# Attention of a pre-norm layer on one core: blocks of 16 queries with 51 keys in place of blocks of 32 with 68, one unit of work per sequence and group

## The chip, the core and the metric

One core of a Trainium2 chip. Its engines are TensorE (PE; the loading of its weights is shown apart as PEld), VectorE (DVE), ScalarE (ACT) and GpSimd (POOL); SyncE (SP) issues all DMAs. Each engine works through its own instructions in order. The metric is the device time of one execution in microseconds. The median of three runs is given, and apart from them one profiled execution, from which all durations come.

## What is computed

A layer for 16 sequences of 256 tokens with 256 channels. Attention has 16 heads of 128 in 4 groups; a group has four query heads and one key and value head. A query sees the 32 newest keys up to itself and the first four of its sequence.

```python
mask = (k <= q) & ((k < 4) | (k >= q - 31))
def attn(x):                                  # x normalised
    q, k, v = x @ wq.T, x @ wk.T, x @ wv.T    # 16, 4 and 4 heads of 128
    scores = einsum('bhtd,bhsd->bhts', q, repeat(k, 4)) / sqrt(128)
    p = exp(where(mask, scores, min) - row_max) * mask
    return einsum('bhts,bhsd->bhtd', p / sum(p), repeat(v, 4)) @ wo.T
x = x + attn(layernorm(x))
x = x + ffn(layernorm(x))     # rows and weights rounded to 8-bit steps, y = x_q @ w_q.T, scaled, + bias
```

All inputs and the output are float32. The four weight matrices of the attention arrive transposed.

## The kernel before

**Units and blocks.** The work of the attention runs in units (n, g, t): sequence, group, and half of the sequence (128 queries). There are 128 of them. A unit has four blocks of 32 queries; a block's four heads give 128 rows of scores. Each block sees 68 keys: the 32 of the block before, its own 32 and the first four. `kt` holds these 68 columns for each block (`keys_to`, L437, four copies on ScalarE), `vw` the matching rows of the values, spread over 96 partitions by DMAs from DRAM (`values_to`, L455).

**What a unit does.** `scores_and_turned` (L561) multiplies queries by keys: one product of 128x128 weights (`qt`) and 68 columns for each block, into `pss`. `mm` (L87) issues every product as two with 64 columns of weights each. VectorE adds the mask (L584) and takes the negative maximum (L586). ScalarE makes four exponentials, 128x68 each (L611), which also give the row sums. VectorE divides (L618, L619, L630) and transposes in 32x32 blocks (L595) into `z`. `z` goes to DRAM (`zd`, L597) and comes back rearranged as `ad` (L601), with keys on 96 partitions. `times_values` (L632) multiplies it by `vw` into `po`, and ScalarE copies `po` to `oT` (L648). The first three units and the last three are turned by TensorE (`ptd`, L578) instead of by way of DRAM.

**Products saved.** Queries, keys, values and the output projection are computed with seven block products in place of eight. GpSimd forms sums of the operands (`left_sums`, `right_sums`, L265 to L275), TensorE multiplies (`products`, L279), and `combine` (L304 to L320) adds the results: on VectorE for queries (`qt`) and the output (`pc`), on GpSimd for keys and values, whose banks ScalarE copies out first (`both_banks`, L333). For queries ScalarE copies one product first (`p_q`, L331). Sequence 0 uses plain products, and so does the output of sequence 15.

**PSUM.** `ps_m` has two banks, which `po`, keys and values and small things share; queries have two (`q0`, `q1`), `py` two, `pss` and `ptd` one each.

**Order.** The loop at L961 goes through the units and writes down each engine's order by hand (`in_written_order`, L21): scores of unit i; products of the output for earlier units; exponentials of i; `po` of the unit whose weights were sent two units ago (`lag`, L854); one of keys or values for the next sequence; division of i; the next queries. Other steps are hung on slots of the loop through `at` (L861): the statistics and transposition of the next sequence (`turned_by_blocks`, L395: four DMAs out, L404, and four back, L413), the FFN of finished sequences (`ffn_steps`, L708), the loads. `hT` (L759) is the FFN's transposed input, copied by ScalarE when its four DMAs `hb` have landed. Before the loop stand the loads (L103 to L115), nine warming products, the first norm, the masks on GpSimd (`mask_steps`), and the first keys, queries and values. After the last unit `last_steps` (L785) does the FFN for the two halves of sequence 15; the first half's steps are placed among the last unit's.

Of the kernel before, what the change touches and what calls it, by code (L numbers as in the profile page):

```python
# [34 lines left out]
def kernel(  # L35
# [25 lines left out]
    QB = 32  # L61
    NBLK = P // QB
    SB = T // QB
    NK = SINK + 2 * QB

    NCH = 3
    NKP = NCH * QB
    assert WIN == QB and HG * QB == P  # L70
# [3 lines left out]
    xp = ctx.enter_context(tc.tile_pool(name="xp", bufs=6))  # L74
# [10 lines left out]
    CT = P // 2  # L85

    def mm(to, left, right, start, stop):  # L87

        for c in range(0, P, CT):
            pe.matmul(to[c : c + CT], left[:, c : c + CT], right, start=start, stop=stop)  # L90

# [14 lines left out]
    wv_sb = const.tile([P, NC, G * D], FP, name="wv_sb")  # L106
    sp.dma_start(wv_sb, wvT.rearrange("(c p) n -> p c n", p=P))
# [4 lines left out]
    for g in range(G):  # L112
        sl = slice(g * HG * D, (g + 1) * HG * D)
        sp.dma_start(wq_sb[:, :, sl], wqT_v[:, :, sl])
    load_x(1)  # L115
# [4 lines left out]
    def other_loads():  # L120

        woT_v = woT.rearrange("(h p) n -> p h n", p=P)
        for g in range(G):
            sp.dma_start(wo_sb[:, g * HG : (g + 1) * HG, :], woT_v[:, g * HG : (g + 1) * HG, :])
        sp.dma_start(wf_sb, wf.rearrange("(c p) d -> p c d", p=P))
        sp.dma_start(bias_bc, bias.partition_broadcast(P))
# [9 lines left out]

    masks = const.tile([P, NT, NBLK, NK], FP, name="masks")
# [4 lines left out]
    floor = const.tile([P, NBLK], FP, name="floor")  # L144
# [4 lines left out]
    def keep(ap, base, cm, step):  # L149

        pool.affine_select(
            out=ap, in_=ap, compare_op=ALU.is_ge, fill=NEG, base=base,
            pattern=[[step, ap.shape[1]]], channel_multiplier=cm,
        )


    scores = [const.tile([P, NBLK, NKP], FP, name=f"scores_{j}") for j in range(2)]
    for j in range(2):
        pool.memset(scores[j], 0.0)

    def mask_steps():


        def build(b):
            pool.memset(masks[:, 0, b, :], 0.0)
            if b < 2:
                pool.memset(masks[:, 0, b, 2 * QB :], NEG)
            if b == 0:
                pool.memset(masks[:, 0, b, 0:QB], NEG)
            for h in range(HG):  # L170
                m = masks[h * QB : (h + 1) * QB, 0, b, 0 : 2 * QB]
                keep(m, QB, 1, -1)
                if b == 1:
                    keep(m[:, SINK:], SINK - 1, -1, 1)
                elif b == 2:
                    keep(m, -1, -1, 1)

        def others():
            like = masks[:, 0, 2:3, :]
            pool.tensor_copy(masks[:, 0, 3:, :], like)  # L180
            pool.tensor_copy(masks[:, 1], like.to_broadcast([P, NBLK, NK]))
            pool.tensor_copy(ident16, ident)
            pool.memset(ones, 1.0)

        return [lambda b=b: build(b) for b in (2, 0, 1)] + [others]
# [22 lines left out]
    def ffn_weight_steps():  # L208
# [23 lines left out]
        def turn():  # L232
            for c in range(NC):
                pt = ps_m.tile([P, NC, P], BF, tag="m", name=f"wt_{c}")
                for o in range(NC):
                    pe.transpose(pt[:, o, :], wq16[:, o, c * P : (c + 1) * P], ident16)
                act.copy(wqfT[:, c, :], pt.rearrange("p o n -> p (o n)"))

        def spread_scales():
            pw = ps_m.tile([P, DM], FP, tag="m", name="pw")  # L240
# [12 lines left out]
    def y_banks(name):  # L253
        return [ps_y.tile([P, NBLK, P], FP, tag=f"y{k}", name=f"{name}_{k}") for k in range(2)]

    def region(p, i):
        return p[REGION[i][0]][:, REGION[i][1]]

    def fast_queries(n, h=0):
        return n > 0 and (n, h) != (B - 1, H - 2)  # L260

    def fast_output(n):
        return 0 < n < B - 1
# [24 lines left out]

    SMALL_FIRST = (4, 5, 3, 1, 2, 6, 7)
    turn_of = [0]

    def q_bank(other, name):
        return ps_q.tile([P, NBLK, P], FP, tag=f"q{turn_of[0] ^ other}", name=name)

    def banks_of_chunk(name):
        p = [ps_m.tile([P, NBLK, P], FP, tag="m", name=f"{name}_0"), q_bank(0, f"{name}_1")]  # L300
        turn_of[0] ^= 1
        return p
# [19 lines left out]
    class Products:  # L322
# [10 lines left out]
        def both_banks(self):  # L333

            copies = [p2.tile([P, 4 - j, P], FP, tag=f"b{j}", name=f"b{j}_{self.tag}") for j in range(2)]
            for k in (1, 0):
# [11 lines left out]

    keys_late = {}
# [19 lines left out]
    def norm_steps(n):  # L369
        def stats():  # L370
            mvs[n] = statistics(xts[n], range(NT), f"a{n}")

        def norm(t):
            if t == 0:
                xns[n] = p1.tile([P, NT, DM], FP, tag="xn", name=f"xn_{n}")
            standardise(xns[n], xts[n], mvs[n], [t])

        return [stats, lambda: norm(0), lambda: norm(1)]
# [7 lines left out]
    def turned(n):  # L386
        xnT[n] = p2.tile([P, NC, T], FP, tag="xnT", name=f"xnT_{n}")
        pt = ps_m.tile([P, NC, T], FP, tag="m", name=f"xt_{n}")
# [5 lines left out]

    def turned_by_blocks(src, pool_of, tag):  # L395


        z = p1.tile([P, NQ, NT * NC, QB], FP, tag="zx", name=f"z_{tag}")
        dve.transpose(z, src.rearrange("p t (c q i) -> p q (t c) i", c=NC, q=NQ))
        zd = dram.tile([P, NQ, NT * NC, QB], FP, tag="zx", name=f"zd_{tag}")  # L400

        def out():
            for a in range(NQ):
                sp.dma_start(  # L404
                    zd[:, a].rearrange("(q j) k i -> j q (k i)", q=NQ),
                    z[a * QB : (a + 1) * QB].rearrange("j q k i -> j q (k i)"),
# [12 lines left out]

    NQ = P // QB  # L420
# [16 lines left out]
    def keys_to(n, g, kb):  # L437

        k = p2.tile([P, 2, SB, NK], FP, tag="kt", name=f"kt_{n}_{g}")
        for e in range(2):  # L440
            kt[n, g + e] = k[:, e]
        act.copy(k[:, :, :, QB : 2 * QB], kb)
        act.copy(k[:, :, 1:, 0:QB], kb[:, :, 0 : SB - 1, :])
        act.copy(k[:, :, 0, 0:QB], kb[:, :, 0, :])
        act.copy(k[:, :, :, 2 * QB :], kb[:, :, 0, 0:SINK].unsqueeze(2).to_broadcast([P, 2, SB, SINK]))

    vws = [const.tile([NKP, SB, 2 * D], FP, name=f"vw_{j}") for j in range(2)]  # L450

    def values_buffer(n, pair):
        vw[n, pair] = vws[pair]

    def values_to(n, pair, v, tiles=range(NT)):  # L455


        w, fresh = vw[n, pair], n == 0
        b0, b1 = tiles[0] * NBLK, (tiles[-1] + 1) * NBLK
        sp.dma_start(w[1:NKP:NCH, b0:b1], v[b0:b1].rearrange("b k d -> k b d"))  # L460
        c1 = min(b1 + 1, SB)
        sp.dma_start(w[0:NKP:NCH, b0 + 1 : c1], v[b0 : c1 - 1].rearrange("b k d -> k b d"))
        if b0 == 0:
            rows = QB if fresh else SINK
            sp.dma_start(w[2 : NCH * (rows - 1) + 3 : NCH], v[0, 0:rows].unsqueeze(1).to_broadcast([rows, SB, 2 * D]))
            if fresh:
                sp.dma_start(w[0:NKP:NCH, 0], v[0])

    def plain_keys(n, g):
        pk = ps_m.tile([P, 2, T], FP, tag="m", name=f"pk_{n}_{g}")  # L470
        for e in range(2):
            for c in range(NC):
                mm(
                    pk[:, e, :], wk_sb[:, c, (g + e) * D : (g + e + 1) * D], xnT[n][:, c, :],
                    start=(c == 0), stop=(c == NC - 1),
                )
        return lambda: keys_to(n, g, pk.rearrange("p e (k i) -> p e k i", i=QB))

    def plain_values(n, t):
        pv = ps_m.tile([P, G * D], FP, tag="m", name=f"pv_{n}_{t}")  # L480
        for c in range(NC):
            mm(
                pv, xnT[n][:, c, t * P : (t + 1) * P], wv_sb[:, c, :],
                start=(c == 0), stop=(c == NC - 1),
            )

        def rest():
            v = p2.tile([P, 3, 2, D], FP, tag="vt", name=f"vt_{n}_{t}")
            act.copy(v[:, 0:2].rearrange("p j e d -> p (j e d)"), pv)
            if t == 0:  # L490
                plain_v.append(dram.tile([T, 2, 2 * D], FP, tag="vp", name=f"vp_{n}"))
                for pair in range(2):
                    values_buffer(n, pair)
            vd = plain_v[0]
            sp.dma_start(vd[t * P : (t + 1) * P].rearrange("p j d -> p (j d)"), v[:, 0:2].rearrange("p j e d -> p (j e d)"))
            for pair in range(2):
                values_to(n, pair, vd[:, pair].rearrange("(b k) d -> b k d", k=QB), [t])
# [4 lines left out]

    def keys(n, pair):

        p = banks_of_chunk(f"pk_{n}_{pair}")
        order = LARGE_FIRST if n > 1 and pair == 0 else SMALL_FIRST
        for to, left, right in products(p, factors(n, wk_sb, wk_sums, pair), order):
            mm(to, left, right, start=True, stop=True)
        k = p1.tile([P, 2, 3, D], FP, tag="ktmp", name=f"ktmp_{n}_{pair}")
        kb = k[:, :, 0:2].rearrange("p e j (k i) -> p e (j k) i", i=QB)  # L510
        rest = lambda: keys_to(n, 2 * pair, kb)
        keys_late[rest] = 1 + pair
        return Products(p, f"k_{n}_{pair}", (k[:, 0, 0:3:2], k[:, 1, 2], k[:, 0, 1], k[:, 1, 0:2])), rest

    def values(n, pair):
        p = banks_of_chunk(f"pv_{n}_{pair}")
# [549 lines left out]
```

## Time and profile before

| | |
|---|---|
| runs, median (lowest to highest) | 753.07 us (751.37 to 756.22), 3 runs |
| profiled execution | 750.27 us, span of its instructions 748.4 us |
| mean granted TensorE clock | 0.994 |
| ScalarE, GpSimd busy | 400.5 us (54%), 519.4 us (69%) |
| HBM | 58.46 MB read, 43.91 MB written |
| packets of DMA, share of 16 engines | 181,144, 47.6% |

A line of a group reads: line of the kernel, engine, operation, output and inputs by their names, partitions x elements of each, how often; then busy time in us, mean of one in ns, and the idle time of the engine just before, with what ended it. TensorE's records of float32 products come in pairs: one product in the program is two records in the trace. A record's duration includes the time through the array, which overlaps with the next one's. Some records are missing, so counts in a stretch are a few per cent low.

The chain of work that ended last, by engine:

```profile
PE 68%; DVE 13%; DMA 8%; POOL 4%; issue 4%; ACT 1%; SPq 1%; ACTq 0%; DVEq 0%; POOLq 0%
```

And the busy tenths of PE and DVE in 40 slices of the span:

```profile
PE   9999999999999999899998998999989899999996
...
DVE  2588898898998988788887996879979799887875
```

### The profile page before, as it was taken

Reading aid. Unit: us, or ns where it says so; the run is one execution under the profiler, and the core shown is the slowest. Engines: PE = TensorE matmul, PEld = TensorE weight load, DVE = VectorE, ACT = ScalarE, POOL = GpSimd, SP = SyncE. Lnnn points to the kernel's source line nnn. Section 1 sums busy time; section 2 is a strip of 40 time slices with the busy share of each in tenths; the row PEclk is TensorE's granted clock in tenths of the full one; section 3 lists DMA queues with packets and bytes.
Section 4 is the critical chain, followed back from the end, with each engine's and each line's share of the span. In section 5 each row is a group of like instructions: output and inputs, shape, how many; then the busy total and the mean of one; then the engine's idle time right before and its main releaser. Section 6 shows DMA issues by size and latency. Waiting matters only on the chain.

```text
span 748.4 us, 31904 instructions
## 1 busy us (share of the span) xinstructions
PE 708.4 (95%) x12916; PEld 671.3 (90%) x12916; DVE 619.6 (83%) x1791; ACT 400.5 (54%) x1575; POOL 519.4 (69%) x814
## 2 busy tenths in 40 slices
PE   9999999999999999899998998999989899999996
PEld 6788899999999999899998997999989899998974
DVE  2588898898998988788887996879979799887875
ACT  3565546555564555546545563555645456455642
POOL 4667977686776777677686774767758677576533
PEclk9999999999999999999999999999999999999998
DMA  6734345454555544555445544455454555454430
GB/s 236 223 117 129 119 136 147 152 141 123 166 140 154 142 134 129 148 148 151 148 107 149 149 137 134 111 149 156 136 158 122 142 145 142 137 144 122 121 111 29
DMA packets 181290, 104.44 MB, mean 140 GB/s; under 512 B 67352, under 2 KB 179352, under 8 KB 181144
## 3 DMA queue, kind: packets, MB, share of 16 engines
q1 hardware_dynamic: 181144, 102.41, 47.6%
q8 instruction: 102, 1.67, 1.0%
q14 instruction: 44, 0.36, 0.2%
HBM read 58.46 MB, written 43.91 MB: 137 GB/s over the span
## 4 chain that ended last, share of the span: by engine, by line
PE 68%; DVE 13%; DMA 8%; POOL 4%; issue 4%; ACT 1%; SPq 1%; ACTq 0%; DVEq 0%; POOLq 0%
PE pq L90 21%; PE py L90 15%; PE po L90 11%; PE pv L90 6%; PE pk L90 6%; PE pss L90 5%; DMA ad<-zd 5%; DVE nmax L586 2%; DVE scores L584 2%; DVE y L775 2%; DMA zd<-z 1%; DMA vd<-vt 1%; DVE qt L316 1%; DVE xs L727 1%; DVE qt L317 1%
## 5 line engine op out<-in xcount | busy, mean ns | idle before, releaser
L611 ACT ACTIVATE scores<-scores,nmax 128x68 f32<-128x68 f32 x512 | 173.6, 340 | 223.1 <-DVE nmax L586 223.0
L90 PE MATMUL po<-ad,vw 96*64 96x128 f32 x2048 | 137.7, 273 | 23.0 <-DMA ad<-zd 12.9
L90 PEld LDWEIGHTS po<-ad,vw 96*64 96x64 f32 x2048 | 118.5, 136 | 31.3 <-ACT scores L611 14.5
L90 PE MATMUL pq<-xs,wq_sums 128*64 128x128 f32 x1428 | 125.6, 273 | 0.0
L90 PE MATMUL pq<-xnT,wq_sb 128*64 128x128 f32 (+1 forms) x1096 | 93.2, 289 | 4.4 <-DVE qt L317 4.3
L611 ACT ACTIVATION_READ_ACCUMULATOR scores<-scores,nmax 128x1 f32 x512 | 95.7, 187 | 0.0
L90 PE MATMUL py<-wo_sb,oT 128*64 128x128 f32 (+1 forms) x1152 | 91.0, 297 | 2.8 <-DVE pc L317 2.6
L90 PEld LDWEIGHTS pq<-xs,wq_sums 128*64 128x64 f32 x1428 | 93.4, 138 | 0.0
L648 ACT COPY oT<-po 128x512 f32<-128x512 f32 x129 | 75.0, 582 | 26.1 <-PE po L90 25.9
L584 DVE SCALAR_TENSOR_TENSOR scores<-pss,masks 128x272 f32<-128x272 f32 x128 | 55.1, 430 | 37.6 <-PE pss L90 36.9
L90 PE MATMUL pss<-kt,qt 128*64 128x68 f32 x2048 | 85.9, 223 | 0.0
L90 PE MATMUL py<-wo_sums,os 128*64 128x128 f32 x1344 | 84.5, 273 | 0.0
L90 PEld LDWEIGHTS pss<-kt,qt 128*64 128x64 f32 x2048 | 81.2, 137 | 1.1 <-issue 0.7
L90 PEld LDWEIGHTS pq<-xnT,wq_sb 128*64 128x64 f32 x1096 | 69.6, 137 | 12.1 <-ACT scores L611 7.1
L90 PEld LDWEIGHTS py<-wo_sb,oT 128*64 128x64 f32 x1152 | 68.4, 137 | 10.6 <-issue 4.3
L266 POOL TENSOR_TENSOR os<-oT 128x256 f32<-128x256 f32 x56 | 44.2, 790 | 43.3 <-ACT oT L648 42.8
L90 PEld LDWEIGHTS py<-wo_sums,os 128*64 128x64 f32 x1344 | 74.1, 137 | 0.0
L595 DVE STREAM_TRANSPOSE z<-scores 128x384 f32<-128x384 f32 x122 | 70.6, 578 | 4.2
L316 POOL TENSOR_TENSOR ktmp<-b_k 128x256 f32<-128x256 f32 x30 | 22.1, 737 | 73.4 <-ACT b_k L337 73.4
L630 DVE TENSOR_TENSOR scores<-scores,sm 128x272 f32<-128x272 f32 x122 | 63.0, 516 | 4.2
L586 DVE TENSOR_REDUCE nmax<-scores 128x4 f32<-128x272 f32 x128 | 55.8, 436 | 4.4
L318 DVE TENSOR_TENSOR qt<-pq,qt 128x256 f32<-128x256 f32 x119 | 50.5, 424 | 4.0
(186 smaller groups left out, 1623.0 us busy)
## 6 DMA issues: line engine op xcount, KB each, us to landing
zd<-z SPq DMA_DIRECT2D x122, 192.0 KB, 2.7
ad<-zd SPq DMA_DIRECT2D x122, 192.0 KB, 2.6
vd<-vt SPq DMA_DIRECT2D x30, 256.0 KB, 2.6
vw<-vd SPq DMA_DIRECT2D x30, 256.0 KB, 3.4
vw<-vd SPq DMA_DIRECT2D x30, 224.0 KB, 3.7
x<-in_x_dram SPq DMA_DIRECT2D x15, 256.0 KB, 4.0
out_dram<-y SPq DMA_DIRECT2D x15, 256.0 KB, 2.1
zd_xnT<-z_xnT SPq DMA_DIRECT2D x56, 64.0 KB, 3.3
```

Of the source, the lines that this page charges most:

```text
L90: pe.matmul(to[c : c + CT], left[:, c : c + CT], right, start=start, stop=stop)
L266: pool.tensor_add(s[0], a21, a22)
L316: eng.tensor_add(c11_u, like(p[0][:, 0:2], c11_u), two(p1, c11_u))
L317: eng.tensor_add(v, like(region(p, 7), v), u)
L318: eng.tensor_add(c21_c22, like(p[1][:, 0:2], c21_c22), v.unsqueeze(1).to_broadcast(c21_c22.shape))
L584: dve.scalar_tensor_tensor(s[:, :, 0:NK], pss, SCALE, masks[:, t], ALU.mult, ALU.add)
L586: dve.tensor_reduce(nmax, s[:, :, 0:NK], AX.X, ALU.max, negate=True)
L595: dve.transpose(z, s.rearrange("p k (c i) -> p c k i", c=NCH))
L611: act.activation(s[:, k, 0:NK], s[:, k, 0:NK], AF.Exp, bias=nmax[:, k : k + 1], scale=1.0, accum_out=sm[:, k : k + 1],)
L630: dve.tensor_mul(s, s, sm.unsqueeze(2).to_broadcast([P, NBLK, NK]))
L648: act.copy(o[:, t, hs].rearrange("p h (k i) -> p k h i", i=QB), po[:, :, hs])
L775: dve.scalar_tensor_tensor(y[:, j, :], pa[:, j, :], xs[:, j : j + 1], wsc_bc, ALU.mult, ALU.mult)
```

## The change

A block becomes 16 queries (four heads: 64 rows) with 51 keys: a window of 47 and the first four. A unit becomes (n, g), the whole sequence: 16 blocks, two side by side. There are 64 places in the loop in place of 128. Scores are 16 products of 64 columns of weights and 51 columns; the products with values are 32, each with 51 rows and 64 columns of weights and 64 columns. The even blocks' weights and values lie on partitions 0 to 50, the odd ones' on 64 to 114, and each kind writes a bank of its own.

```diff
-    QB = 32
+    QB = 16
+    NW = QB + WIN - 1
+    NK = NW + SINK
-    xp = ctx.enter_context(tc.tile_pool(name="xp", bufs=6))
+    xp = ctx.enter_context(tc.tile_pool(name="xp", bufs=5))
...
+    def unit_scores(i):
+        n, g = units[i]
+        pss = ps_s.tile([P, NK2, NK], FP, tag="s", name=f"pss_{n}_{g}")
+        for k in range(NK2):
+            for j in range(NJ):
+                b = NJ * k + j
+                t, bt = divmod(b, NB // NT)
+                pe.matmul(
+                    pss[j * HALF : (j + 1) * HALF, k, :], qt[i][:, t, bt].rearrange("p h i -> p (h i)"),
+                    kt[n, g // 2][:, g % 2, b, :], start=True, stop=True,
+                )
+        s = ss[i] = scores[i % 2]
+        dve.scalar_tensor_tensor(s[:, :, 0:NK], pss, SCALE, masks, ALU.mult, ALU.add)
...
+        dve.tensor_reduce(nmax, s[:, :, 0:NK], AX.X, ALU.max, negate=True)
...
+    def normalised(i, sm):
...
+        dve.tensor_mul(s[:, :, 0:NK], s[:, :, 0:NK], sm.unsqueeze(2).to_broadcast([P, NK2, NK]))
+        z = p1.tile([P, NCH, NK2, BL], FP, tag="z", name=f"z_{n}_{g}")
+        dve.transpose(z, s.rearrange("p k (c i) -> p c k i", c=NCH))
...
+        sp.dma_start(zd, z.rearrange("p c k i -> p (c k i)"))
+        def back():
...
+            for j in range(NJ):
+                src = zd[j * HALF : (j + 1) * HALF].rearrange("(a x) (c r) -> c x a r", a=2, c=NCH)
+                for c in range(NCH):
+                    p0 = j * HALF + c * BL
+                    sp.dma_start(ad[p0 : p0 + BL].rearrange("p a k y -> p a (k y)"), src[c])
...
+    def times_values(i):
...
+        po = [ps_m.tile([P, NK2, HALF], FP, tag="m", name=f"po_{n}_{g}_{j}") for j in range(NJ)]
+        for k in range(NK2):
+            for j in range(NJ):
+                r = slice(j * HALF, j * HALF + NK)
+                for d0 in range(0, D, HALF):
+                    v0 = g % 2 * D + d0
+                    pe.matmul(
+                        po[j][d0 : d0 + HALF, k].rearrange("p (a y) -> p a y", a=2),
+                        w[r, k, v0 : v0 + HALF], ad[r, :, k], start=True, stop=True,
+                    )
```

Every unit now goes through DRAM; there is no `ptd`. The keys are laid in one line with 32 zeros ahead (`k_line`), from which ScalarE copies 16 overlapping windows of 47 (`keys_to`, two copies of 1,504 and 128 columns in place of four); the values come back in six DMAs for each pair of groups in place of three (`values_to`). Keys and values use both banks of `ps_m`, queries both of theirs. Masks are built on 16 partitions by four steps of GpSimd and spread by eight DMAs. The small FFN products use the bank that `ptd` had.

The order of the loads at the start: `x` of sequence 0, `wk`, the first quarter of `wq`, `wv`, then the eight DMAs of the masks and two stores of the first values, and only then `other_loads`: the other three quarters of `wq`, `x` of sequence 1, `wo` and the rest.

The loop is written anew. `at(place, point, step)` hangs the other steps on named points, which `do` runs:

```python
    def values_place(i):
        return i + 2 if i < U - 3 else i + 1
    def output_place(i):
        return values_place(i) + 1 if units[i][0] < B - 1 else values_place(i) + (i < U - 1)
    for i in range(PLACES):
        do(i, "load")                       # DMAs of x, of xn and h on their way
        ways.pop(i - 1)()                   # four DMAs: ad of unit i - 1
        stores                              # six DMAs: vw
        exps, sm = unit_scores(i)
        do(i, "gap")                        # DVE: statistics, y, one half of xn
        both banks of the last keys or values copied (ACT) and combined (POOL)
        do(i, "pool"); do(i, "narrow")      # sums of xn on POOL; hT on ACT
        first = queries(i + 1, 0)           # PE
        exps(range(2)); first.first(); exps(range(2, NK2)); first.combine(dve)
        projected_fast(o, 0)                # PE: output of unit o = i - 3
        do(i, "early")                      # DVE: the other half of xn, rounding of h
        values_out = [times_values(o) ...]  # PE: po of unit i - 2
        ways[i] = normalised(i, sm)         # DVE, then the DMA of z
        copied(); summed()                  # ACT: oT; POOL: its sums
        second = queries(i + 1, 1); second.first()
        projected_fast(o, 1); second.combine(dve)
        keys_to (ACT) or the store of the values
        waiting = start_chunk(i)            # PE: keys or values of the next sequence
        do(i, "linear"); do(i, "late"); do(i, "leave")
    last_steps(0), then last_steps(1)
```

(That is the loop at L946 of the changed kernel, shortened, with what each line does.) For a sequence whose last output stands in place p, the FFN's steps stand in p+1 (statistics, `h`), p+2 (scale, rounding, transposition), p+3 (DMAs out at its start, back at its end), p+4 (`hT`, product) and p+5 (`y`, stored). The line numbers of the steps change: mask and maximum are L568 and L570, exponentials L575, division L583 to L586, transposition L589, `oT` L623, `hT` L744.

## Prediction

> **What bounds the kernel now.** I read the page's busy shares first, then the groups by form, then single places in the timeline. The profiled execution took 750.27 us, its span is 748.4 us; the median of the three runs is 753.07 us, 0.37% above it. All sums below are of the span.
>
> ```profile
> PE 708.4 (95%) x12916; PEld 671.3 (90%) x12916; DVE 619.6 (83%) x1791; ACT 400.5 (54%) x1575; POOL 519.4 (69%) x814
> ```
> TensorE is busy for 95%, so its work is the bound; VectorE is next. The seven starts of line 727 (184.6, 229.0, 273.4, 319.9, 364.2, 411.0, 458.9) put a sequence in the steady part at 45.7 us on average, 44.3 at best.
>
> ```profile
> L611 ACT ACTIVATE scores<-scores,nmax 128x68 f32<-128x68 f32 x512 | 173.6, 340 | 223.1 <-DVE nmax L586 223.0
> L90 PE MATMUL po<-ad,vw 96*64 96x128 f32 x2048 | 137.7, 273 | 23.0 <-DMA ad<-zd 12.9 <-issue 8.0 <-DMA zd<-z 1.5
> L90 PE MATMUL pss<-kt,qt 128*64 128x68 f32 x2048 | 85.9, 223 | 0.0
> L595 DVE STREAM_TRANSPOSE z<-scores 128x384 f32<-128x384 f32 x122 | 70.6, 578 | 4.2
> L630 DVE TENSOR_TENSOR scores<-scores,sm 128x272 f32<-128x272 f32 x122 | 63.0, 516 | 4.2
> L586 DVE TENSOR_REDUCE nmax<-scores 128x4 f32<-128x272 f32 x128 | 55.8, 436 | 4.4
> L584 DVE SCALAR_TENSOR_TENSOR scores<-pss,masks 128x272 f32<-128x272 f32 x128 | 55.1, 430 | 37.6 <-PE pss L90 36.9
> ```
> In these groups by form the numbers behind the bar are busy us, mean ns of one, idle us before. Of TensorE's idle time some 21 us lie before `po`, waiting for the weights' way through DRAM.
>
> ```profile
> 403.05 0.67 PE L90 MATMUL pss<-kt,qt 128*64 128x68 f32 x16
> 410.48 1.51 PE L90 MATMUL py<-wo_sums,os 128*64 128x128 f32 x24
> 18.96 0.64 PE L90 MATMUL pss<-kt,qt 128*64 128x68 f32 x16
> 19.53 0.39 PEld L578 LDWEIGHTS ptd<-ident,z 128*96 128x96 f32 x4
> 20.11 3.22 PEld L90 LDWEIGHTS pq<-xnT,wq_sb 128*64 128x64 f32 x32 [0.18 <-issue]
> ```
> The timeline (start, duration, engine) gives the real rate: 24 records of 128 columns last 1.51 less one tail of 0.27, 54.7 ns each; 16 of 68 columns, 29.5 ns each. The single starts show why: the two 64-column halves run at the same time (two `pss` start at 19.316 and 19.322, the next two at 19.375 and 19.381), so one half takes 109 ns for 128 columns, 59 for 68, hence 56 for 64 and 45 for 51. Two weight loads of one half follow at 55 ns at the closest (405.583, 405.638). A change of tile shape costs about 0.145 us: the last `pss` product streams to 19.44 (19.381 plus 0.059), and the first `ptd` product has its load at 19.58 (the next load follows at 19.577); on the way back the loads idle 0.18.
>
> **The change, part by part.** Scores: 2,048 records again (16 products a place, two records each, 64 places), now 51 columns. A half needs 55 ns (its load, not its 45 ns of columns): 27.5 against 29.5 ns, 3.5 us a sequence against 3.8; bounds 22.5 and 29.5.
>
> Products with values: 4,096 records of 64 columns for 2,048 of 128. No row shows a tile of 64 rows. If the two row halves run side by side as the column halves do, a record costs 56/4 = 14 ns, 3.6 us a sequence; if they take turns, 28 ns, 7.1 us, today's 7.0; if the new shape runs one tile at a time, 55 ns, 14 us. I take 14, because the column halves, the nearest row, overlap fully and the row halves write separate banks; the others stay in the range. Eight changes of shape a sequence add 1.2 us.
>
> The Trainium skill (TensorE: Matmul & The Clock Gate, Back-to-back issue gap) speaks against it: up to 64 columns a matmul costs about 60 cycles, some 25 ns, however few they are. By that rule `po` is estimated at 256 x 25 ns = 6.4 us a sequence, and the span, by the walk through the places below, at 743; this trace's starts 6 ns apart contradict it as a limit across tiles.
>
> All else on TensorE stays: 560 records of 54.7 ns and 0.4 us of bfloat16, 31.1 a sequence. Work a sequence: 41.9 before, 39.4 after. The rest of 45.7 was idle, and the waits of `po` for DRAM go, as a place is twice as long and the lag stays two places; 16 `ad` issues for 8 and 12 `vw` for 6 hide there too, one place (10 us) to spare.
>
> VectorE: elements cost 1.04 ns (291 ns for 128, 424 for 256 at lines 317, 318), so the 408-wide steps cost 0.57, 0.58 and 0.58 (440 ns plus 141), the transposition 0.67 (line 399's row). 64 of each for 128 save about 90 us of busy time (244.5 less 64 x 2.4), but not of span: all is now one chain in a place twice as long. ScalarE keeps 512 exponentials, one every 0.33 us (0.34 now); the two `kt` copies at lines 436 and 437 move 1,632 columns at 0.81 ns (275 ns for 128, 586 for 512), 1.7 us, like today's four. GpSimd keeps its steps: 32.8 us a sequence in the windows, hidden under 43.
>
> A plain place, from the first score product, in us: scores to 0.88; sum and maximum 1.1 to 2.27; two exponentials to 3.0, `p_q` to 3.3, six more to 5.3. VectorE forms the first half of the next queries 3.4 to 5.1, weights and their transposition 5.45 to 7.15, the second half 7.2 to 8.9. TensorE: queries to 2.4, `py` to 3.7, `po` with two shape changes to 4.9, second queries to 6.5, `py` to 8.2, keys or values to 9.7. So 9.7, TensorE-bound, VectorE 0.8 behind. The four places of a sequence (i mod 4 = 1, 2, 3, 0):
>
> 1: 9.7.
> 2: `hT` is copied by ScalarE ahead of the exponentials, and its four `hb` DMAs stand on SP behind six `vw` and `zd`. SP: `xnT` back (2.60), `zd_hb` (1.85), four `ad` (1.3), six `vw` (3.1), `zd`, then `hb` issued 8.65 to 11.25 of place 1 and landing 2.6 later, 4.05 into this place. Exponentials wait from 2.4 to 4.7, the first query combination starts at 5.7, second queries (two banks, freed one after the other) end at 8.15, `py` 9.9, values and FFN product 11.9.
> 3: VectorE does xn, y and the statistics (2.6) before that combination: from 4.95; queries end 7.4, place 10.7. Its late steps (xn turned, h) end 1.7 into the next place.
> 0: so the sum starts at 1.75, quantising adds 1.45, the second half ends at 10.6; the scores wait for it: 10.7.
> Sum 43.0 a sequence.
>
> Head: the scores start at 15.2 as now (14.6), but `wq`'s last three quarters stand on SP behind eight `masks` DMAs and `vp`, which wait for GpSimd and ScalarE: issued at 16.5, landed 19.6, TensorE idle 3.4. `x` of sequence 1 lands at 23, VectorE waits for it in order, `z` of place 0 is late (27.8), 12 `vw` issues stand before `ad`: `po` can start at 40 where TensorE is ready at 35.7, and place 2's scores have lost 2.5. Place 3 starts at 44.4; place 3 itself 10.7, plain `py` in 4 to 6 adds 1.3. Today's TensorE has no gap over 0.6 us there.
>
> Tail, from place 62: 52.9. Place 62 takes 13.8 (two `po` in turn through the same two banks). In place 63 the FFN's steps stand before the last weights (VectorE 9.4 to 11.1), which go through DRAM (today through TensorE) and reach `po` at 17.6; `py` ends 23.9, the FFN product 24.4, then both last halves one after the other (5.3 and 8.2, today's durations; today they overlap with the last unit): 39.1. TensorE is idle for 25 of it, today for about 11.
>
> Span: 44.4 + 10.7 + 1.3 + 14.5 sequences (58 places) x 43.0 + 52.9 = 733. With the 1.9 outside the span and the median's 0.37%, 738. Head and tail cost about 25, so the change pays only where a sequence is under 44.1.
>
> **Rivals.** *Row halves take turns* (28 ns): `po` ends 0.9 later; plain places 10.6, place 0 10.7, 2 and 3 unchanged (VectorE, ScalarE): 43.9 a sequence, 746, in runs 751: no change. For it: no 64-row tile in the trace. Against it: the independent column halves.
>
> *`hT` in time.* If SP runs ahead so that `hb` lands before 2, place 2 takes 10.2: 41.3 a sequence, 708, in runs 713. For it: in the list of waits ScalarE waited for `hb` once, 3.6 us. Against it: today the copy stands further back in ScalarE's order (403.51, its last `hb` issue at 399.82), and the sum above has `hb` 1.65 after place 2's `hT` is due.
>
> *The chain is the bound* (slower). Three of four places end by VectorE and ScalarE, not TensorE; rows' means hide longer ones: line 630 takes 516 ns on average, 440 in the places I read; line 734 594 against 440. At 10% on the some 9 us of chain: 0.9 each in 2, 3, 0 and 0.2 in 1, 45.9 a sequence, 775, in runs 780. It decides from 44.1 a sequence, 4% more. Against it: most rows I used are at their medians.
>
> **How the numbers follow.** Forecast 0.38 (724 to 752 alone), turns 0.20, `hT` in time 0.12, chain 0.30 (760 to 800). Over 1% is what a measurement tells from no change: 745.5 and 760.6. Faster: 0.28 + 0.02 + 0.12 = 0.42; same 0.09 + 0.13 + 0.02 = 0.24; slower 0.34. Range 712 to 784 leaves out some 0.06 below and 0.1 above (with one tile at a time, over 800).
>
> **What would show it.** `po` starts: four within 56 ns (14) or two. `pss` pairs 55 ns apart. Line 727's starts 43.0 apart. ScalarE's `hT` waiting some 2 us on `hb` each sequence. No wait of `po` on `ad` but in places 2 and 64. TensorE idle 3 to 4 us at 16 and at 36, and about 6 before the last `po`. If TensorE's busy share falls below 85% in the steady part while the period is above 44, the chain has won; if VectorE's steps at lines 568, 570, 586 leave 0.57 to 0.6, my slope is wrong.

## The result, and the profile after

The changed kernel takes 1436.11 us (median of 4 runs, 1434.61 to 1438.21), the kernel before beside it 752.22 (749.02 to 756.22): 1.909 times as long, 95% interval 1.899 to 1.919. The forecast was 738, the range 712 to 784.

First the page of the changed kernel: busy time with its share of the span, the granted TensorE clock in 40 slices, DMA packets of the one big queue (count, MB, share of 16 engines), and the chain of work that ended last, by engine and by line.

```profile
span 1432.8 us, 35739 instructions
PE 758.0 (53%) x14952; PEld 704.8 (49%) x14952; DVE 535.9 (37%) x1417; ACT 394.5 (28%) x1506; POOL 516.1 (36%) x795
...
PEclk9569776777767787676777767777776777767766
...
q1 hardware_dynamic: 153440, 96.13, 23.1%
...
SPq 43%; DMA 32%; PE 16%; DVE 2%; issue 2%; ACT 2%; POOL 1%; ACTq 0%; DVEq 0%; POOLq 0%
SPq L456 36%; DMA vw<-vd 28%; PE pq L90 6%; PE po L613 4%; PE py L90 4%; SPq L599 4%; ACT scores L575 2%; PE pk L90 2%; DMA zd<-z 1%; SPq L451 1%; PE pss L563 1%; SPq L457 1%; DMA hb<-zd_hb 1%; SPq L404 1%; DMA x<-in_x_dram 1%
```

No compute engine is the bound any more: TensorE's share fell from 95% to 53%, and the chain is 43% SyncE's issuing and 32% transfers. Two names hold nearly all of that: line 456, one of the three lines that issue copies of `vw`, and the landing of `vw`. Yet the DMA engines move fewer packets than before (153,440 for 181,144) and are busy for 23.1% of their time on average. The mean clock is 0.737 (before 0.994).

The groups by form, in the prediction's order (busy us, mean ns, idle us before and what ended it):

```profile
L575 ACT ACTIVATE scores<-scores,nmax 128x51 f32<-128x51 f32 x512 | 166.1, 327 | 91.8 <-DVE nmax L570 91.8
L613 PE MATMUL po<-ad,vw 51*64 51x64 f32 x4096 | 113.7, 267 | 619.7 <-DMA vw<-vd 557.7 <-DMA ad<-zd 53.5 <-ACT scores L575 4.9
L589 DVE STREAM_TRANSPOSE z<-scores 128x512 f32<-128x512 f32 x64 | 45.5, 712 | 256.3 <-DMA zd<-z 254.7
L570 DVE TENSOR_REDUCE nmax<-scores 128x8 f32<-128x408 f32 x64 | 37.0, 578 | 2.2
L568 DVE SCALAR_TENSOR_TENSOR scores<-pss,masks 128x408 f32<-128x408 f32 x64 | 37.1, 579 | 112.2 <-PE pss L563 112.2
```

The steps themselves have the durations that were forecast (0.33, 0.58, 0.58; the transposition 0.71 for 0.67). What is new is 558 us in which `po` waits for `vw`. SyncE's timeline in one place (start, duration) shows the source:

```profile
597.87 0.24 SPq L451 DMA_DIRECT2D vw<-vd  x1
598.15 10.04 SPq L456 DMA_DIRECT2D vw<-vd  x1
608.23 0.41 SPq L457 DMA_DIRECT2D vw<-vd  x1
608.69 0.33 SPq L451 DMA_DIRECT2D vw<-vd  x1
609.06 14.06 SPq L456 DMA_DIRECT2D vw<-vd  x1
623.16 0.31 SPq L457 DMA_DIRECT2D vw<-vd  x1
623.58 0.34 SPq L591 DMA_DIRECT2D zd<-z  x1
```

The DMAs shown take 0.2 to 0.4 us to issue, but line 456's take 10 and 14, four times a sequence. This is not that line's own work: it copies 16 or 32 rows of one block, and the same copy takes 0.39 us (median) in the split kernel below, where it is line 457. It stands behind line 451, which is issued in 0.24 and 0.33 us and copies a window of 47 rows by seven blocks, 1 KB each: 329 packets. The single packets of the trace say how they run. From 612 to 622 us, 23 packets of 1 KB start in each microsecond, one after the other:

```
start us   612.029  612.071  612.113  612.157  612.203  612.245
took ns    46       46       47       49       46       46
```

43.5 ns apart, and the DMA share from 612 to 622 is 0.07 of sixteen engines: one DMA engine works, while fifteen stand still. 329 x 43.5 ns is 14.3 us a copy, and two copies follow each other on that engine; the last data land at 628.9, 31 us after the first copy was issued. Until the engine has worked off enough of a copy, SyncE is held at the next DMA, which is line 456's. In the kernel before, the copies of 32 rows (256 KB) landed in 3.4.

The starts of the places (first score product; means over places 8 to 59) put it beside the prediction's walk. The last two columns are experiments below.

| us | forecast | changed | split 32+15 | `zd_hb` later |
|---|---|---|---|---|
| place i mod 4 = 1 | 9.7 | 9.81 | 9.83 | 9.83 |
| 2 | 11.9 | 37.09 | 17.44 | 10.88 |
| 3 | 10.7 | 10.83 | 10.84 | 10.84 |
| 0 | 10.7 | 28.21 | 9.94 | 9.95 |
| a sequence | 43.0 | 85.9 | 48.1 | 41.5 |
| place 3 starts at | 44.4 | 101.2 | 55.4 | 54.4 |
| from place 62 to the end | 52.9 | 99.2 | 55.9 | 58.4 |

The excess stands in places 2 and 0, the first that use new values.

### The profile page after: what moved, and what is told of

Read it like the earlier page. It is cut to its first block, busy times and chain, and to the rows that moved or that the text cites. A ratio compares the mean times of both kernels' runs of the same rounds, so it can differ in the third digit from the quotient of the medians.

```text
span 1432.8 us, 35739 instructions
## 1 busy us (share of the span) xinstructions
PE 758.0 (53%) x14952; PEld 704.8 (49%) x14952; DVE 535.9 (37%) x1417; ACT 394.5 (28%) x1506; POOL 516.1 (36%) x795
## 2 busy tenths in 40 slices
DMA packets 153600, 98.41 MB, mean 69 GB/s; under 512 B 69792, under 2 KB 143456, under 8 KB 153440
## 3 DMA queue, kind: packets, MB, share of 16 engines
q1 hardware_dynamic: 153440, 96.13, 23.1%
HBM read 59.18 MB, written 36.70 MB: 67 GB/s over the span
## 4 chain that ended last, share of the span: by engine, by line
SPq 43%; DMA 32%; PE 16%; DVE 2%; issue 2%; ACT 2%; POOL 1%; ACTq 0%; DVEq 0%; POOLq 0%
SPq L456 36%; DMA vw<-vd 28%; PE pq L90 6%; PE po L613 4%; PE py L90 4%; SPq L599 4%; ACT scores L575 2%; PE pk L90 2%; DMA zd<-z 1%; SPq L451 1%; PE pss L563 1%; SPq L457 1%; DMA hb<-zd_hb 1%; SPq L404 1%; DMA x<-in_x_dram 1%
## 5 line engine op out<-in xcount | busy, mean ns | idle before, releaser
L613 PE MATMUL po<-ad,vw 51*64 51x64 f32 x4096 | 113.7, 267 | 619.7 <-DMA vw<-vd 557.7
L613 PEld LDWEIGHTS po<-ad,vw 51*64 51x64 f32 x4096 | 99.7, 176 | 637.8 <-issue 603.8
L310 DVE TENSOR_TENSOR qt<-pq,p_q 128x256 f32<-128x256 f32 x120 | 48.7, 406 | 423.9 <-ACT p_q L325 423.8
L575 ACT ACTIVATE scores<-scores,nmax 128x51 f32<-128x51 f32 x512 | 166.1, 327 | 91.8 <-DVE nmax L570 91.8
L623 ACT COPY oT<-po 128x512 f32<-128x512 f32 x128 | 67.9, 581 | 345.6 <-PE po L613 315.2
L589 DVE STREAM_TRANSPOSE z<-scores 128x512 f32<-128x512 f32 x64 | 45.5, 712 | 256.3 <-DMA zd<-z 254.7
L90 PE MATMUL pq<-xnT,wq_sb 128*64 128x128 f32 (+1 forms) x1088 | 109.0, 332 | 31.3 <-DVE qt L311 25.4
L744 ACT CAST hT<-hb 128x512 bf16<-128x512 f32 x14 | 8.6, 617 | 370.1 <-DMA hb<-zd_hb 370.1
L575 ACT ACTIVATION_READ_ACCUMULATOR scores<-scores,nmax 128x1 f32 x512 | 96.6, 189 | 0.0
L90 PEld LDWEIGHTS py<-wo_sums,os 128*64 128x64 f32 x1344 | 89.6, 155 | 0.0
L568 DVE SCALAR_TENSOR_TENSOR scores<-pss,masks 128x408 f32<-128x408 f32 x64 | 37.1, 579 | 112.2 <-PE pss L563 112.2
L563 PE MATMUL pss<-kt,qt 128*64 128x51 f32 x2048 | 71.3, 223 | 9.1 <-ACT kt L437 7.2
L563 PEld LDWEIGHTS pss<-kt,qt 128*64 128x64 f32 x2048 | 68.5, 139 | 13.4 <-ACT kt L437 10.3
L436 ACT COPY kt<-k_line 128x1504 f32<-128x1504 f32 x32 | 47.0, 1470 | 34.7 <-POOL k_line L314 34.6
```

The lines of the kernel that those rows point to most:

```text
L90: pe.matmul(to[c : c + HALF], left[:, c : c + HALF], right, start=start, stop=stop)
L310: eng.tensor_add(c11_u, like(p[0][:, 0:2], c11_u), two(p1, c11_u))
L436: act.copy(k[:, :, :, 0:NW], windows())
L563: pe.matmul(pss[j * HALF : (j + 1) * HALF, k, :], qt[i][:, t, bt].rearrange("p h i -> p (h i)"), kt[n, g // 2][:, g % 2, b, :], start=True ...
L575: act.activation(s[:, k, 0:NK], s[:, k, 0:NK], AF.Exp, bias=nmax[:, k : k + 1], scale=1.0, accum_out=sm[:, k : k + 1],)
L589: dve.transpose(z, s.rearrange("p k (c i) -> p c k i", c=NCH))
```

## The experiments

**One engine, or something else?** The theory: with 47 rows the whole copy goes to one DMA engine. Rivals: the amount or placement of the data makes it slow, or TensorE does. Two kernels change only how the 47 rows are cut; a third puts the suspected fault into the kernel before.

```diff
-            sp.dma_start(w[r : r + NW, 1:], ...)               # 47 rows
+            for lo, hi in ((0, 32), (32, NW)):                 # second kernel: ((0, 46), (46, 47))
+                sp.dma_start(w[r + lo : r + hi, 1:], ...)      # DRAM address + lo rows
```

> The changed kernel, the copy of 47 value rows (line 456) sent as two, of 32 and of 15 rows: the same packets, bytes and places, two DMAs more for each pair of groups. Theory 'one engine': 47 rows put all 329 packets of 1 KB on one DMA engine, one after the other at 43.5 ns (14.3 us a copy, SyncE held for 10 to 14 us); with 32 and 15 rows they spread, each copy lands in some 3 to 4 us, SyncE's issue falls under 1 us and the time falls to what the prediction's walk gave without this, 738 us (712 to 784). Rival 'amount': the copies are slow because each DRAM row is read three times or because they are unaligned in the partitions: nothing changes, above 1350 us. Rival 'TensorE': products in 64-row tiles or the lower clock (0.74) take the time, the copies only wait for them: above 1000 us with SyncE still ahead.

(The copy of 47 rows that is cut is line 451; line 456, which this expectation names, is the one held behind it.) Measured: 810.35 us beside 754.82 for the kernel before, ratio 1.075 (1.068 to 1.082). Of the 684 us above the kernel before 626 are gone with the same bytes (HBM read 59.18 MB in both), so amount, placement and 64-row products fall. The copy behind is no longer held for long:

```profile
413.83 0.39 SPq L457 DMA_DIRECT2D vw<-vd  x1
...
415.46 1.87 SPq L457 DMA_DIRECT2D vw<-vd  x1
```

But 810 is above the range; the rest had another cause.

> The same with 46 and 1 rows. 'One engine', in its form 'as many engines as the largest divisor of the row count up to 16': 46 rows use two engines, 161 packets each (7.0 us), the single row one engine (7 packets). The first copy of a pair holds SyncE for some 2.7 us and the second for some 7 (about 100 packets of an engine seem to find room ahead, 10.0 us of issue for 14.3 of data), some 20 us a sequence where the changed kernel has 49: the time lies between, 800 to 1000 us. If only prime or odd row counts are slow, it is that of the split 32 and 15 (some 740). 'Amount': above 1350.

Measured: 999.66 us in one run, the upper edge of what was expected. SyncE's timeline (the two copies of 46 and 1 rows of one line together):

```profile
507.85 3.73 SPq L452 DMA_DIRECT2D vw<-vd  x2
511.63 0.42 SPq L457 DMA_DIRECT2D vw<-vd  x1
512.11 0.30 SPq L458 DMA_DIRECT2D vw<-vd  x1
512.46 6.67 SPq L452 DMA_DIRECT2D vw<-vd  x2
```

The first pair's two copies apart, from the chain of waits:

```profile
507.85 0.29 SPq L452
508.14 0.04 issue
508.18 3.40 SPq L452
```

The 46 rows are issued in 0.29 us; SyncE is then held at the single row behind them, for 3.4 us and in the second pair for 6.4, where 2.7 and 7 were expected; and 46 to 47 packets of 1 KB start in each microsecond from 514 to 519, two at a time. 46 is not prime and still slow: the largest divisor up to 16 counts, 2 for 46 and 1 for 47.

For the third kernel, one of the value copies of the kernel before (32 rows by eight blocks) is cut:

```diff
-        sp.dma_start(w[1:NKP:NCH, b0:b1], v[b0:b1].rearrange("b k d -> k b d"))
+        for lo, hi in ((0, QB - 1), (QB - 1, QB)):             # 31 rows, 1 row
+            sp.dma_start(w[1 + lo * NCH : 1 + (hi - 1) * NCH + 1 : NCH, b0:b1], ...)
```

> The kernel before, with its copy of 32 value rows by 8 blocks sent as 31 and 1 rows. 'One engine': 248 packets at 43.5 ns, 10.8 us, in place of about 0.7; landing 13 us after its issue where it was 3.4, SyncE held for some 6.5 us each time, 30 times; the time rises by 20 to 80 us (770 to 830), since the values are used two units after they are sent and the wait is hidden in part. 'Amount' and 'TensorE': no change, 753.

Measured: 1060.37 us in one run, 306 above the kernel before: the mechanism is there, its price in the whole is nearly four times the upper end of what was expected. SyncE is held for 7 us, as expected, at the single row behind the 31:

```profile
397.84 0.67 SPq L461
398.51 0.05 issue
398.56 7.00 SPq L461
...
407.04 5.91 DMA ad<-zd
```

This is the chain of waits. The expectation counted only the wait for `vw`; but here the `ad` that comes next stands on SyncE behind the held copy, and it lands 5.9 us after its issue (2.6 in the kernel before), while packets of 1 KB still start one after the other until 412. `po` waited 252 us for `ad`, in 31 waits.

> The changed kernel with each copy of 47 rows sent as 44 and 3. By the rule 'largest divisor of the row count up to 16': 44 rows go over eleven engines (28 packets each, 1.2 us), 3 rows over three; as good as 32 and 15: 805 to 820 us. By 'only multiples of 16 are spread': 44 rows on four engines or fewer, 77 packets or more each (3.3 us a copy), 830 to 1000 us.

Measured: 807.32 us in one run, like 32 and 15. The Trainium skill (DMA: Bandwidth & Descriptors, section on why a DMA increments its semaphore by 16) states this rule: the largest number up to 16 that divides the slowest dimension of both sides. The cuts agree with it as far as their packets show. By the rule 47 rows go on one engine (a packet every 43.5 ns), 46 on two (two at a time) and 44 on eleven; with 44, 62 and 65 packets of 1 KB start in the two quarters of a microsecond from 413.25, where eleven engines at 43.5 ns would start 63. For 32 and 15, by the rule sixteen and fifteen engines, only the time was read.

**What holds the split kernel at 810?** One place of four, 17.4 us. ScalarE and TensorE there (line numbers are one higher than in the changed kernel):

```profile
420.72 1.35 PE L614 MATMUL po<-ad,vw 51*64 51x64 f32 x60 [0.71 <-DMA vw<-vd]
...
425.05 0.62 ACT L745 CAST hT<-hb 128x512 bf16<-128x512 f32 x1 [8.60 <-DMA hb<-zd_hb]
425.57 0.33 ACT L576 ACTIVATE scores<-scores,nmax 128x51 f32<-128x51 f32 x1
...
427.36 0.75 PEld L90 LDWEIGHTS pq<-xnT,wq_sb 128*64 128x64 f32 x8 [5.43 <-ACT p_q L325]
```

The place starts at 415.75. The exponentials could start at 418.2 and stand in ScalarE's order behind `hT`, whose data come at 425.0; TensorE then waits 5.4 for ScalarE. And there is a second cost. The same eight weight loads take 0.42 in the places without a wait, here 0.75. The busy time by stretch shows why (stretch, its length, busy us and instructions of PE, PEld, DVE, ACT and POOL, then the granted clock, the DMA share and GB/s):

```profile
415.75:422.00 6.25, 5.54 (x152) 5.17 (x148) 2.03 (x6) 0.63 (x2) 2.83 (x6) 1.00 0.69 133
422.00:427.36 5.36, 0.08 (x3) 0.00 (x0) 0.72 (x3) 2.31 (x13) 0.98 (x3) 0.86 0.33 77
427.36:431.00 3.64, 3.60 (x34) 3.64 (x36) 3.23 (x10) 2.25 (x10) 1.50 (x3) 0.50 0.00 0
```

After the wait TensorE runs at half clock. First repair: `hT` behind the exponentials; the rival repair: `hb` earlier on SyncE.

```diff
-  ("narrow", 4, "narrow"), ("linear", 4, "linear")
+  ("narrow", 4, "linear"), ("linear", 4, "linear")      # hT later
...
-  ("back", 3, "leave")
+  ("back", 3, "mid")                                    # other kernel: hb between ad and vw
```

> The split 32 and 15, and ScalarE's copy hT moved from before the exponentials of its place to the place's end, just ahead of the FFN product. Theory 'hT': the 72 us by which the split kernel (810) lies above the forecast are the exponentials waiting behind hT for hb in one place of four (17.4 us there, 11.9 forecast; the other three as forecast). hb lands 8.6 into the place, the product needs hT at some 10: the place falls to about 10.7, a sequence from 48.0 to some 41.2, the span by 14 x 6.8 = 95 to some 713, 716 in runs. Rival 'queue': SyncE's eight vw and the late vw themselves hold that place; then it stays above 14 and the time above 765.

Measured: 752.78 beside 755.45, ratio 1.001 (0.995 to 1.006). 58 us are gone, not 95: the place takes 12.75, some at 11.8, some at 14.2. So `hT` was most of it and the rival a part.

> The split 32 and 15, hT where it was, but hb's four DMAs put on SyncE ahead of the vw DMAs of their place and not behind them. hb lands about 5 us earlier, some 2.5 to 4 into the place, so hT no longer holds the exponentials for more than 1 to 2 us. If SyncE's order is the whole of it: some 720. If vw, now 2.6 us later, is next late (po waited for it 0.7 to 2.5 already), the place is about 13.3 and the time some 750.

Measured: 813.88 us in one run, no gain at all: more than its worse case. The wait for `hb` fell from 96.7 to 32.0 us in sum, the wait of `po` for `vw` rose from 19.6 to 56.4:

```profile
426.35 0.33 PE L614 MATMUL po<-ad,vw 51*64 51x64 f32 x4 [2.35 <-DMA vw<-vd]
429.18 2.01 PE L614 MATMUL po<-ad,vw 51*64 51x64 f32 x60 [2.49 <-DMA vw<-vd]
```

(This place starts at 420.06.) What was taken from one transfer went to the next in the same queue, and `po` runs at half clock after it (2.01 for 60 records, where 64 take 1.16 in the undisturbed places). So the queue is the cause behind both waits: SyncE issues `xnT`, `zd_hb`, `ad` and then `vw` in the place before. In the kernel with `hT` later, the two kinds of place by stretch, the slow one first:

```profile
306.05:313.00 6.95, 5.04 (x128) 4.76 (x128) 5.23 (x15) 3.46 (x19) 3.54 (x7) 0.97 0.74 170
313.00:316.40 3.40, 3.40 (x61) 3.28 (x57) 0.66 (x2) 1.34 (x3) 1.90 (x4) 0.55 0.52 126
...
395.42:402.40 6.98, 5.70 (x158) 5.36 (x156) 5.25 (x15) 3.72 (x20) 3.54 (x7) 1.00 0.77 141
402.40:407.40 5.00, 5.00 (x96) 5.00 (x94) 3.73 (x11) 2.66 (x7) 3.63 (x7) 1.00 0.56 173
```

In the first, `po` waited 1.9 us for `vw` and the clock fell for 3.4; in the second it waited 1.3 and the clock stayed. The repair for that: `zd_hb` behind `vw`.

```diff
-  ("out", 3, "load")
+  ("out", 3, "gap")
```

> The kernel with hT later (split 32 and 15), and the four DMAs of zd_hb put on SyncE behind the eight vw of their place in place of ahead of ad. Theory: what is left in that place (12.75 on average where the plain ones have 9.85) is po waiting for vw, whose DMAs stand behind xnT's four, zd_hb's four and ad's four; the wait is 1.3 to 2 us, and where it makes TensorE idle long enough its clock is 0.5 for some 3.4 us more. vw 2 us earlier lands before po is due: the place falls to some 10.8, the clock of 0.5 goes from the steady part, and the time falls by 14 x 1.9 = 27 us to some 726. Rival: hb, now later, is late for the FFN product in its turn; then the place stays at 12 to 13 and the time at 745 to 755.

Measured: 725.59 beside 756.19, ratio 0.959 (0.953 to 0.964); the place takes 10.88. `po` no longer waits, and `hT` waits 2 us where nothing stands behind it that is due:

```profile
300.37 1.23 PE L614 MATMUL po<-ad,vw 51*64 51x64 f32 x64
306.53 0.62 ACT L745 CAST hT<-hb 128x512 bf16<-128x512 f32 x1 [2.02 <-DMA hb<-zd_hb]
```

**Do these repairs help with 47 rows whole?**

> The changed kernel with its copies of 47 rows whole, but with hT and zd_hb moved as in the two last repairs, which took 85 us off the split kernel. 'One engine is the bound': that engine has 4 x 14.3 us of these copies a sequence and, from the page, 23.1% of 16 engines' span less the copies, spread evenly, some 17 us more: 74 us of the 86 a sequence took; while a sequence can't go below 74, SyncE held for 49 stays, and the moves bring little: 1380 to 1440 us, and not under 1200. Rival: the moves are worth 85 us here too, 1350 or less.

Measured: 1402.05 us in one run: 34 us, not the 85 that the same two moves are worth in the split kernel. With 47 rows whole, their copies set the time; whether the loaded engine does it or SyncE held behind it, this run does not tell.

**Head and tail.** First the order of the loads; then, besides, the last two halves of the FFN placed alternately; then both with the queue repaired and two further moves.

```diff
     load_wq(0); wv
+    load_wq(1), (2), (3)                  # were in other_loads, behind the masks
-    at(0, "load", other_loads)            # wq, x 1, wo, x 2, wf, bias
+    at(0, "load", other_loads)            # x 1, x 2
+    at(1, "leave", later_loads)           # wo, wf, bias; the FFN weights' steps one place later
...
-    for f in last_steps(0): f()
-    for f in last_steps(1): f()
+    for steps in zip(last_steps(0), last_steps(1)):
+        for f in steps: f()
```

> The kernel with hT later, and the first loads in another order: wq's last three quarters ahead of the masks, wo, the FFN's weights and the bias only after the first ad. Theory: in the split kernel place 3 starts at 55.4 where the prediction had 44.4, because the first z and vw stand on the DMA engines behind 2 MB of wo, and TensorE waits 5.2 for wq. Both gone, place 3 starts at 38 to 44: 11 to 17 us less than with hT later alone. If these were not the cause: no change.

Measured: 754.97 us in one run, no gain in the time. Place 3 starts at 48.4, 6.6 earlier than with `hT` later alone (55.0); the same run lost more in the places i mod 4 = 2, 13.88 on average for 12.75. Half a hit: the head was as described, but worth 7 us, not 11 to 17.

> The same, and the FFN's steps of the last sequence's two halves placed alternately in place of one half after the other (tiles of their own for the second half). By the prediction's durations (5.3 and 8.2 one after the other) some 4 to 5 us less than with the head alone: about 697 in all, below the kernel before (753) by some 7%.

Measured: 743.13 beside 755.45, ratio 0.982 (0.977 to 0.987), where 697 was expected: the place that waits for `vw` was still there. What the tail alone is worth is not separated here.

> The same in the kernel with the head and the tail altered, and two further moves: the first sequence's values of the second pair of groups (eight DMAs) go out one place later, behind the first ad; and in the last place the FFN's scale and rounding of sequence 14 come behind the last weights. Expected by the sum: 743 less 27 for the place, 6 for the first ad, 2 for the last weights, some 708 (700 to 718), 6% below the kernel before.

Measured: 717.80 beside 756.19, ratio 0.951 (0.947 to 0.954): the fastest, 4.9% under the kernel before, at the upper edge of what was expected. Place 3 starts at 43.7, but then takes 16.1, as its `po` waits 3.8 for an `ad` issued behind `wo`: of 11 us gained in the head 6 go back. TensorE is the bound again:

```profile
PE 670.0 (94%) x14952; PEld 623.3 (87%) x14952; DVE 539.7 (76%) x1417; ACT 391.5 (55%) x1506; POOL 525.5 (74%) x795
...
PEclk9979999999999999999999999999999999999897
```

## Why the prediction was wrong

**The step that failed** is the sentence "16 `ad` issues for 8 and 12 `vw` for 6 hide there too, one place (10 us) to spare", and in place 2's walk "six `vw` (3.1)". They counted DMAs and took their issue from copies of 32 rows. The copy of 47 rows has no row in the trace of before; it was neither named as unknown nor bounded. It occupies one engine for 14.3 us and holds SyncE at the next DMA for 10 to 14, four times a sequence: 624 of the 700 us between the forecast span (733) and the measured one (1432.8), by the split. None of the rivals was this one.

**`hT`'s wait** was the right mechanism with a size too small: `hb` landing 4.05 into place 2 was forecast (4.15 by the terms given there), 9.3 was measured with the split kernel. SyncE's walk was some 5 us short: the four `ad` took 2.8 us for 1.3, eight `vw` 5.1 for 3.1, and `hb` was issued 13.4 to 15.9 into place 1, not 8.65 to 11.25. And the half clock after a wait was in no term of the sum. Places 3 to 61 together are 62 us over the walk.

**The head** was right in its parts and 11 us short (place 3 at 55.4 for 44.4). In the split kernel TensorE waits 5.2 us for `wq` (3.4 forecast); the DMA engines are full from 20 to 31 us, with 2 MB of `wo` among the loads; `x` of sequence 1 lands at 25.4 (forecast 23), the first `z` goes out at 31.6 (27.8). The repaired orders got 7 to 11 us of it; which load costs how much was not separated. **The tail**: 55.9 for 52.9.

These three sum up: 11 + 62 + 3 = 76, and 733 + 76 = 809 is the split kernel's 808.4.

**TensorE's terms held.** The row halves run side by side. In the split kernel the `po` products start so:

```
410.033 410.039 410.046 410.053   410.091 410.098 410.104 410.111
```

Four within 20 ns, the next four 58 ns later: 14.6 ns a record, 14 forecast. The gap of 25 ns that the prediction cites is no limit across tiles, and the rival *row halves take turns* (28) falls. `pss` pairs follow at 58 ns, 55 forecast. The changes of shape, VectorE's slope and ScalarE's pace stand as well; places 1 and 3 are within 0.2 us of the walk, place 0 is 0.8 shorter.

***`hT` in time*** was a rival with 41.3 us a sequence; with `hT` and `zd_hb` moved the kernel takes 41.5, and its span is 724.6, not 708, since head and tail are 16 longer than in the walk. ***The chain is the bound*** (slower by 10% longer steps) had the sign right, and the cause wrong: the steps are no longer than forecast. (Its 440 ns for line 734 stands in no record of the kernel before; the shortest takes 478.)

Of the signs listed, one was missing: a wait of `po` on `vw`. The list watched `ad`, which was hidden but for one wait in place 2 (53.5 us), where one was forecast. And one sign misleads: TensorE busy under 85% with a period above 44 us was to mean that the chain has won. It came out so (53%, 85.9 us), yet the steps of the chain kept their durations; that sign cannot tell long steps from late data.

Not tried: how much of the lost time was SyncE held, and how much the late data; and what the lower clock cost by itself.

## What to carry to other kernels

When a change alters the shape of a DMA, not only its number, it is a new operation: price it from a row with the same row count, or bound it with one engine carrying it all (here 43.5 ns for each 1 KB), before anything is said to hide it. Cut a prime row count into parts that divide well: two DMAs of 32 and 15 rows instead of one of 47 were worth 626 us. In a queue that issues in order, walk every DMA from the place before; moving one forward makes the next one late, and only moving something out that nobody needs soon (here `zd_hb`) gains.

## What the runs showed of the hardware

A copy that loads one engine holds SyncE at the next DMA. The 47 rows are issued in 0.22 to 0.34 us; the copy behind them is held for 10.0 us where the engine was free before, for 14.1 where the copy before was still running. By an estimate from these numbers some 100 of the 329 packets find room ahead ((14.3 - 10.0) us / 43.5 ns), and SyncE waits for the rest. Behind 46 rows on two engines (161 packets on each, 7.0 us of data) it was held for 3.4 and 6.4 us, behind 31 rows on one (248 packets, 10.8 us) for 7.0.

TensorE's clock halves after short waits: after 1.9 us for 3.4 us, after 5.4 us for 6.8 (425.85 to 432.67 in the split kernel); after 1.3 us it did not. The Trainium skill (TensorE: Matmul & The Clock Gate, Part 1) puts the limit at an idle window of about 3.4 us; the length of the slow stretch agrees, the 1.9 us of waiting are shorter than its window, and the measurement decides. The length of a wait alone does not decide, though: in the kernel with `hT` later one of 1.7 us (at 132.7) was followed by a slow stretch, one of 1.86 us (at 222.3) by none. Five slow stretches there last 3.41 us each and start at 135.14, 179.51, 268.26, 312.63 and 357.00, always a multiple of 3.413 us apart; on that grid the 1.86 us fall into two windows, as 1.6 and 0.3. So where a wait falls seems to matter as much as how long it is; no run here moved a wait to show it.

A mean clock of 0.737 at 1.0 or 0.5 means half speed for 53% of the span (2 x 0.263). So a wait of TensorE that is followed by such a stretch costs more than itself.
